# Twenty score passes of a unit, split as twelve and eight where other work follows

## The chip, the core and the metric

The program runs on one core of one Trainium2 chip. The metric is the device time of one launch in microseconds (us), the median of three runs. The profile comes from one more execution. The core has a TensorE (PE, with its weight loads listed as PEld), a VectorE (DVE), a ScalarE (ACT), a GpSimd (POOL) and a SyncE (SP) that issues most DMAs.

## The reference

Eight sequences of 1024 tokens with 256 channels go through a block of three layers, each added to its own input: half a feed-forward layer with eight routed experts, an attention layer, and the same feed-forward layer again. The attention is where the change lies.

```python
xd = (x @ W_down).reshape(b, t, h, s)              # 16 heads of 16 channels
keys    = einsum('bthk,hik->bthi', xd, tokeys) * scale
queries = einsum('bthk,hik->bthi', xd, toqueries) * scale
values  = einsum('bthk,hik->bthi', xd, tovalues)
dot  = einsum('bqhs,bkhs->bhqk', queries, keys)
attn = softmax(dot, axis=-1)
out  = einsum('bhqk,bkhs->bqhs', attn, values).reshape(b, t, e) @ W_unify + b_unify
...
x = x + 0.5 * ffn(layernorm(x))
x = x + attention(layernorm(x))
x = x + 0.5 * ffn(layernorm(x))
```

## The kernel before, in words

**Pairs and units.** `attention` works on 32 pairs: a pair is one sequence with one group of four heads. A pair has 16 units. A unit is one block of 512 queries with one block of 128 keys. The four heads of a group sit on the four strips of 32 rows of TensorE's array (`r = slice(32 * h, 32 * h + 32)`), so four matmuls, one in each strip, can run beside each other.

**Score passes.** In a unit, `passes` issues twenty matmuls of 512 columns (line 985). Each head has three "s" passes into a bank `psc` of PSUM: the high part of the keys, the low part, and one that subtracts the row maximum through `ones_r`. After the third, ScalarE takes the exponential of the bank into a tile `ex` (line 994). Each head also has two "m" passes into a bank `pm`. They are the scores of the next pair; VectorE reduces them to a maximum in `halves` (line 1001). Below, s0 to s3 and m0 to m3 name the bank and the pass by head; three passes in a row with the name s0 are the three passes of that bank.

**Order on TensorE.** The list `ORDERS` gives the twenty passes in two halves of ten: first `s0 s1 m2 m3 s0 s1 m2 m3 s0 s1`, then the same with `s2 s3 m0 m1`. Four names in a row that use four strips are a round. Each half is two whole rounds and a round of two.

**Weighing.** `weigh` multiplies the four `ex` tiles of the unit before with the values into one bank `av` (line 1016). These matmuls use all 128 rows and 32 columns each, so they cannot share the array with the strips. A weighing is done whole, between the two halves of passes, or in two parts of 256 columns: one between the halves, the other at the end.

**Other work.** `beside` is a list of generators that prepare the next sequence (`prepare`: transposes `ptan`, projections `pxd`, `pq`, `pv`), finish the last (`unify`: `pu`) and route it (`route`: transposes `ptrn`, logits `pl`, and in `places` the small matmuls `places` and `behind`). `run` advances them with `step`. In some units, by `SLOTS_OF`, it takes a step of kind `ARRAY` at the end of the unit, behind both halves; then `other` is true and the weighing is whole. This is called a mixed unit here, and any other a plain unit. 156 of the units are mixed: 28 with a `pu` step, 28 with `pxd`, 14 with `pq`, 14 with `pv`, 14 with `ptan`, 13 with `ptrn`, 24 with `pl`, 6 with `places`, 6 with `behind`, and 9 whose step issues nothing on TensorE. Ahead of 116 of them is a plain unit, ahead of the other 40 a mixed one.

**Banks.** `psc` and the tiles `ptan`, `ptrn`, `pxd`, `pq`, `pv` (by `bank`) share four PSUM banks. `pm`, `pu`, `pl`, `places` and `behind` (by `bank_v`) share three. A bank is taken in turn, and its first matmul waits for the reader of the tile that had it: ScalarE's `ex` or copy, or VectorE's reduction. TensorE, ScalarE and VectorE run their instructions in the order in which the kernel writes them (`tc.manual_schedule`); POOL and SP are scheduled by the tile layer.

The lines that decide what a unit does, in `run`:

```python
passes(n, n + 1, u, ORDERS[0], todo)
other = u % TB in slots[0] and due(ARRAY) is not None
whole = other or u % TB < 2
weighed((0, 1) if whole else (0,))
passes(n, n + 1, u, ORDERS[1], todo)
if other:
    step(ARRAY)
elif not whole:
    weighed((1,))
```

Of the kernel before, what the change touches and what calls it, by code (L numbers as in the profile page):

```python
# [40 lines left out]
def macaron(  # L41
# [714 lines left out]
    def reload(b):  # L756
        load_x(b, after_first.rearrange("(b t) d -> b t d", t=T))

    def attention(use, weights, router):
# [16 lines left out]
        ORDERS = [  # L776
            [(kind, int(h)) for kind, h in order.split()] for order in (
                "s0 s1 m2 m3 s0 s1 m2 m3 s0 s1", "s2 s3 m0 m1 s2 s3 m0 m1 s2 s3"
            )
        ]  # L780


        ORDER_OF_LAST = [("s", h) for _ in range(3) for h in range(4)]

        def bank(name):

            return use.sc.tile([P, 512], F32, tag="sc", name=name)

        def bank_v(name):

            return use.pm.tile([P, 512], F32, tag="pm", name=name)
# [125 lines left out]
        def fetch(n):  # L917

            b, g = divmod(n, G)
            rows = slice(g * 64, (g + 1) * 64)  # L920
            qt = qts[n] = use.pool.tile([P, T], F32R, tag=f"q{n % 3}", name=f"q_{n}")
            kt = kts[n] = use.pool.tile([P, 2, T], F32R, tag=f"k{n % 3}", name=f"k_{n}")
            for i in range(2):
                nc.sync.dma_start(
                    out=kt[:, i, :].bitcast(F32), in_=krows[b][i, rows].rearrange("r c t -> (r c) t")
                )
            nc.sync.dma_start(out=qt.bitcast(F32), in_=qrows[b][rows].rearrange("r c t -> (r c) t"))
# [26 lines left out]
        def passes(n, m, u, order, todo):  # L954

            q, c = divmod(u, TB)
            t, half = divmod(u, 2)
            qs, ks = slice(q * 512, (q + 1) * 512), slice(c * P, (c + 1) * P)  # L960

            def in_order(row):

                return row[:, qs].rearrange("p (t a j) -> p a t j", t=4, a=4)

            qm, km = slice(t * P, (t + 1) * P), slice(half * 512, (half + 1) * 512)
            for kind, h in order:
                if (n if kind == "s" else m) is None:
                    continue
                r = slice(32 * h, 32 * h + 32)  # L970
                if (kind, h) not in todo:
                    if kind == "s":
                        todo[kind, h] = bank(f"psc_{n}_{u}_{h}"), [
                            (kts[n][r, 0, ks], in_order(qts[n][r])),
                            (kts[n][r, 1, ks], in_order(qts[n][r])),
                            (ones_r[r, :], ms[(2 * n + q) % 4][r, :]),
                        ]
                    else:
                        todo[kind, h] = bank_v(f"pm_{m}_{u}_{h}"), [
                            (qts[m][r, qm], kts[m][r, i, km]) for i in range(2)  # L980
                        ]
                    todo[kind, h, "of"] = len(todo[kind, h][1])
                ps, left = todo[kind, h]
                lhs, rhs = left.pop(0)
                nc.tensor.matmul(  # L985
                    ps, lhsT=lhs, rhs=rhs,
                    start=(len(left) + 1 == todo[kind, h, "of"]), stop=not left,
                )
                if left:
                    continue  # L990
                if kind == "s":
                    ex = use.pool.tile([P, 512], F32, tag="ex", name=f"ex_{n}_{u}_{h}")

                    nc.scalar.activation(ex, ps, AF.Exp, scale=S ** -0.5)  # L994
                    todo["ex", h] = ex
                else:
                    if m not in halves:
                        halves[m] = use.pool.tile(
                            [P, TB, 2, 4], F32, tag="halves", name=f"halves_{m}"
                        )  # L1000
                    nc.vector.tensor_reduce(  # L1001
                        halves[m][:, t, half, h : h + 1], ps, AX.X, ALU.max, negate=True
                    )
# [3 lines left out]
        def weigh(n, u, exs, parts=(0, 1)):  # L1007

            b, g = divmod(n, G)
            q, c = divmod(u, TB)  # L1010
            if (n, q) not in avs:
                avs[n, q] = use.av.tile([P, 512], F32, tag="av", name=f"av_{n}_{q}")
            cols = slice(256 * parts[0], 256 * (parts[-1] + 1))
            for h, ex in enumerate(exs):
                at = (c * HEADS + 4 * g + h) * V
                nc.tensor.matmul(  # L1016
                    avs[n, q][32 * h : 32 * h + 32, cols],
                    lhsT=vps[b % 2][:, at : at + 2 * S],
                    rhs=ex[:, cols],
                    start=(c == 0),  # L1020
                    stop=(c == TB - 1 and parts[-1] == 1),
                )
            if c == TB - 1:
                divide(n, q)
# [90 lines left out]
        def stats(b):  # L1115

            sl = slice(b * TB, (b + 1) * TB)
            yield from norm_steps(f"a{b}", b, amean[:, sl], arstd[:, sl])
# [4 lines left out]
        def afterwards(n=0):  # L1123

            for _ in range(len(later) - n):
                later.pop(0)()
# [5 lines left out]
        def due(kind):  # L1132
            return min((w for w in beside if w[1] == kind), key=lambda w: w[0], default=None)
# [29 lines left out]
        def ones(i):  # L1163
            vp = use.pool.tile([P, TB * HEADS * V + S], F32, tag=f"vp{i}", name=f"vp{i}")
            nc.gpsimd.memset(vp, 1.0)
            vps.append(vp)

        def zero_rows(i):
            m = use.pool.tile([P, 512], F32R, tag=f"m{i}", name=f"m{i}")
            nc.gpsimd.memset(m.bitcast(F32), 0.0)  # L1170
            ms.append(m)
# [46 lines left out]
        def run(own):  # L1218
            for i in range(2, 4):
                zero_rows(i)  # L1220
            fetch(1)
            ones(1)
            for b in range(AHEAD - 1, B):
                reload(b)
                beside.append([G * (b - 1) - 1, DVE, stats(b)])
            last = None

            def weighed(parts=(0, 1)):
                if last is not None:
                    weigh(*last, parts=parts)  # L1230

            for n in range(PAIRS):
                ahead = n + 1 < PAIRS
                if n == (B - 1) * G:
                    done_by(n)
                    use.pool = own
                    use.last.close()
                    router.open()

                queue(n)  # L1240
                for u in range(UNITS):
                    todo = {}
                    old = len(later)
                    slots = SLOTS_OF[n % G < 2]
                    if ahead:
                        passes(n, n + 1, u, ORDERS[0], todo)

                        other = u % TB in slots[0] and due(ARRAY) is not None

                        whole = other or u % TB < 2  # L1250
                        weighed((0, 1) if whole else (0,))
                        passes(n, n + 1, u, ORDERS[1], todo)
                        if other:
                            step(ARRAY)
                        elif not whole:
                            weighed((1,))
                    else:

                        passes(n, None, u, ORDER_OF_LAST, todo)
                        weighed()  # L1260
                        other = False
                        if u > 1:
                            step(ARRAY)
                        if u == TB + 3:
                            beside.append([n + 1, ARRAY, islice(unify(B - 1), 2)])
                    if u % TB in slots[1]:
                        step(DVE)
                    if not other:
                        step(POOL)
                    last = (n, u, [todo["ex", h] for h in range(4)])  # L1270
                    afterwards(len(later) - old)
                    if ahead and u % TB == TB - 1:
                        lowest(n + 1, u // TB)
                if ahead:
                    done_by(n)
            weighed()
            afterwards()
            done_by(PAIRS + G)
            for _ in unify(B - 1, TB // 2):
                pass  # L1280
# [124 lines left out]
```

## Time and profile before

| what | value |
|---|---|
| time, median of 3 runs (lowest, highest) | 2952.49 us (2950.14, 2956.28) |
| time of the profiled execution | 2947.41 us |
| its span, first to last instruction | 2945.7 us |
| mean granted TensorE clock | 0.978 |
| busy: PE, PEld, DVE, ACT, POOL | 2805.4, 1549.6, 1879.2, 1375.5, 863.4 us |
| line 1001, reductions of `pm` | 2048, mean 681 ns |
| line 994, exponentials of `psc` | 2048, mean 596 ns |
| line 985, passes into `psc` (two kinds) and `pm` | 4096 + 2048 and 4096 |
| line 1016, weighings | 6472, mean 450 ns |

The profiled execution is 5.1 us below the median, and 1.7 us of its time lie outside the span. The mixed units begin between 670 and 2389 us of the span. The starts of matmuls are read from the trace; their ends are modelled, so the distance from one start to the next says more than a duration.

### The profile page before, as it was taken

How to read it: one execution, taken by the hardware profiler on the slowest of the kernel's cores; microseconds unless marked ns; L12 is line 12 of the kernel's file. 1: busy time of each engine (PE TensorE's matmuls, PEld its weight loads, DVE VectorE, ACT ScalarE, POOL GpSimd, SP SyncE). 2: the span in 40 equal slices, each digit the busy share in tenths (PEclk: the TensorE clock that was granted, in tenths of full speed). 3: DMA queues.
4: the chain of work that ended last, by engine and by line, in shares of the span. 5: the costliest groups of instructions: out<-in, count | busy, mean ns of one | idle time of the engine just before them, and what ended most of it. 6: DMA issues, size and time to landing. Idle time of an engine off the chain costs nothing.

```text
span 2945.7 us, 56665 instructions
## 1 busy us (share of the span) xinstructions
PE 2805.4 (95%) x22066; PEld 1549.6 (53%) x22066; DVE 1879.2 (64%) x4177; ACT 1375.5 (47%) x2512; POOL 863.4 (29%) x1144
## 2 busy tenths in 40 slices
PE   4799999899999999999999999999999998999998
PEld 4567776454444444444444444444444445666775
DVE  7344223567998888888888787788787963222221
ACT  1111111207666666766766766766765672111111
POOL 3444433314001034133123221321410215432331
PEclk7799999999999999999999999999999999999999
DMA  8522553415112101301301301301411102311440
GB/s 227 149 85 76 184 186 99 152 38 177 35 49 77 67 27 64 117 24 58 126 24 56 127 24 50 133 24 44 161 38 38 39 3 71 129 60 51 148 148 28
DMA packets 163736, 251.46 MB, mean 85 GB/s; under 512 B 36737, under 2 KB 109698, under 8 KB 163458
## 3 DMA queue, kind: packets, MB, share of 16 engines
q1 hardware_dynamic: 144178, 196.93, 20.6%
q0 software_dynamic: 18432, 50.62, 5.1%
q8 instruction: 177, 2.90, 0.4%
q14 instruction: 101, 0.83, 0.1%
q10 hardware_dynamic: 848, 0.18, 0.0%
HBM read 144.10 MB, written 103.57 MB: 84 GB/s over the span
## 4 chain that ended last, share of the span: by engine, by line
PE 63%; DVE 13%; issue 1%; POOL 1%; DMA 0%; ACT 0%; POOLq 0%; ACTq 0%
PE psc L985 19%; PE av L1016 15%; DVE halves L1001 9%; PE pm L985 7%; PE pe_o L499 5%; PE ph_o L456 5%; PE pe_e L499 2%; PE ph_e L456 2%; PE pu L1061 2%; PE pxd L860 2%; PE pv L892 1%; DVE turned L1031 1%; PE pq L878 1%; PE pl L1089 1%; PE ptrn L830 0%
## 5 line engine op out<-in xcount | busy, mean ns | idle before, releaser
L1001 DVE TENSOR_REDUCE halves<-pm 128x1 f32<-128x512 f32 x2048 | 1309.7, 681 | 258.1 <-PE pm L985 229.0
L994 ACT ACTIVATE ex<-psc 128x512 f32<-128x512 f32 x2048 | 1111.6, 596 | 579.1 <-PE psc L985 574.4
L985 PE MATMUL pm<-k,q 32*128 32x512 f32 x4096 | 872.5, 449 | 47.3 <-DVE halves L1001 38.0
L985 PE MATMUL psc<-q,k 32*128 32x512 f32 x4096 | 794.1, 456 | 2.9 <-PEq L668 2.9
L1016 PE MATMUL av<-ex,vp 128*32 128x256 f32 (+1 forms) x6472 | 614.2, 450 | 0.0
L985 PEld LDWEIGHTS psc<-q,k 32*128 32x128 f32 x4096 | 327.8, 183 | 480.5 <-issue 421.5
L985 PEld LDWEIGHTS pm<-k,q 32*128 32x128 f32 x4096 | 375.5, 184 | 129.8 <-DVE halves L1001 107.1
L985 PE MATMUL psc<-m,ones_r 32*128 32x512 f32 x2048 | 407.9, 390 | 0.0
L456 PE MATMUL ph_o<-bT_o,oa 128*128 128x512 f32 x704 | 321.9, 607 | 9.6 <-DVE h_o L474 8.5
L499 PE MATMUL pe_o<-ob,h_o 128*128 128x256 f32 x1408 | 318.6, 382 | 0.0
L1039 POOL TENSOR_TENSOR ot<-turned,rec 128x256 f32<-128x256 f32 x64 | 39.6, 619 | 886.6 <-DVE rec L1034 880.1
L499 PEld LDWEIGHTS pe_o<-ob,h_o 128*128 128x128 f32 x1408 | 265.5, 191 | 47.2 <-issue 13.5
L1016 PEld LDWEIGHTS av<-ex,vp 128*32 128x32 f32 x6472 | 129.0, 108 | 299.3 <-issue 276.3
L456 PEld LDWEIGHTS ph_o<-bT_o,oa 128*128 128x128 f32 x704 | 133.1, 194 | 164.1 <-issue 149.8
L470 ACT ACTIVATE h_o<-ph_o,ob 128x512 f32<-128x512 f32 x88 | 60.4, 687 | 338.7 <-PE ph_o L456 319.5
L474 DVE TENSOR_SCALAR h_o<-ph_o,ob 128x512 f32<-128x512 f32 x88 | 66.0, 750 | 230.4 <-ACT h_o L470 226.0
L985 PEld LDWEIGHTS psc<-m,ones_r 32*128 32x128 f32 x2048 | 197.7, 185 | 13.3
L509 DVE SCALAR_TENSOR_TENSOR y_o<-pe_o,old_o 128x256 f32<-128x256 f32 x88 | 37.2, 423 | 195.2 <-PE pe_o L499 195.1
L499 PE MATMUL pe_e<-wb,h_e 128*128 128x256 f32 (+1 forms) x640 | 143.9, 381 | 0.0
L456 PE MATMUL ph_e<-bT_e,wa 128*128 128x320 f32 x512 | 140.6, 433 | 1.8 <-ACT bT_e L204 1.8
L204 ACT COPY bT_o<-pt_bT_o 128x1024 f32<-128x1024 f32 x22 | 22.3, 1012 | 241.2 <-PE pt_bT_o L200 241.2
L499 PEld LDWEIGHTS pe_e<-wb,h_e 128*128 128x128 f32 (+1 forms) x640 | 112.9, 179 | 16.4 <-issue 3.1
(181 smaller groups left out, 2395.8 us busy)
## 6 DMA issues: line engine op xcount, KB each, us to landing
k<-krows SPq DMA_DIRECT2D x64, 512.0 KB
wa<-in_w_dram SPq DMA_DIRECT2D x16, 1024.0 KB
wb<-in_w_dram SPq DMA_DIRECT2D x16, 1024.0 KB
krows<-kh SPq DMA_DIRECT2D x32, 512.0 KB
krows<-kl SPq DMA_DIRECT2D x32, 512.0 KB
q<-qrows SPq DMA_DIRECT2D x32, 512.0 KB
rows_o<-buf SPq DMA_DIRECT2D x88, 130.0 KB
x<-in_x_dram SPq DMA_DIRECT2D x8, 1024.0 KB
```

The lines of the kernel that those rows point to most:

```text
L456: nc.tensor.matmul(ps[:, i * 512 : i * 512 + width], lhsT=wa[:, k, (m + i) * P : (m + i + 1) * P], rhs=xnt[:, k, c0:c1], start=(k == 0), s ...
L470: nc.scalar.activation(t[:, 0, : hi - lo], ps[:, lo - c0 : hi - c0], AF.Relu, bias=bias[:, m : m + 1],)
L474: nc.vector.tensor_scalar(t[:, 1, : hi - lo], ps[:, 512 + lo - c0 : 512 + hi - c0], bias[:, m + 1 : m + 2], 0.0, ALU.add, ALU.max,)
L499: nc.tensor.matmul(ps[lo - i * P : hi - i * P, :D], lhsT=of[:, lo - a : hi - a], rhs=w[:, m, :], start=(m == 0), stop=(m == MC - 1),)
L509: nc.vector.scalar_tensor_tensor(y[:n, :], ps[:n, :D], 0.5, olds[i][:n, :], ALU.mult, ALU.add)
L860: nc.tensor.matmul(ps, lhsT=wd_sb[:, k, m * P : (m + 1) * P], rhs=xnt[:, k, :], start=(k == 0), stop=(k == KC - 1),)
L985: nc.tensor.matmul(ps, lhsT=lhs, rhs=rhs, start=(len(left) + 1 == todo[kind, h, "of"]), stop=not left,)
L994: nc.scalar.activation(ex, ps, AF.Exp, scale=S ** -0.5)
L1001: nc.vector.tensor_reduce(halves[m][:, t, half, h : h + 1], ps, AX.X, ALU.max, negate=True)
L1016: nc.tensor.matmul(avs[n, q][32 * h : 32 * h + 32, cols], lhsT=vps[b % 2][:, at : at + 2 * S], rhs=ex[:, cols], start=(c == 0), stop=(c == ...
L1039: nc.gpsimd.tensor_tensor(outs_t[q][:, :, at : at + S].rearrange("p (t a) s -> p a t s", t=4), by[:, :, :S].rearrange("p (a t) s -> p a t ...
L1061: nc.tensor.matmul(ps[:, i * D : (i + 1) * D], lhsT=outs[b, g, q][:, at : at + P], rhs=wu_sb[:, g, :], start=(g == 0), stop=(g == G // 2 - 1),
```

## The change

Mixed units get an order list of their own. Their first half has twelve passes in three rounds of four strips, their second half eight passes in two rounds; the whole weighing stays between the halves and the step behind them. The order in plain units stays. `other` is now worked out ahead of the first half, because the choice of the list needs it; nothing in between changes what it depends on.

```diff
+        ORDERS_WITH_OTHER = [
+            [(kind, int(h)) for kind, h in order.split()] for order in (
+                "s2 s3 m0 m1 s2 s3 m0 m1 s2 s3 s0 s1", "s0 s1 m2 m3 s0 s1 m2 m3"
+            )
+        ]
...
                     if ahead:
-                        passes(n, n + 1, u, ORDERS[0], todo)
 
                         other = u % TB in slots[0] and due(ARRAY) is not None
+                        orders = ORDERS_WITH_OTHER if other else ORDERS
+                        passes(n, n + 1, u, orders[0], todo)
 
                         whole = other or u % TB < 2
                         weighed((0, 1) if whole else (0,))
-                        passes(n, n + 1, u, ORDERS[1], todo)
+                        passes(n, n + 1, u, orders[1], todo)
```

## The prediction

> **What bounds the kernel now.** I read the page, the busy times by stretch and then the timeline of single units. Attention fills 655 to 2396 us:
>
> ```profile
> 655.00:2396.00 1741.00, 1696.71 (x17253) 787.07 (x17255) 1451.50 (x2855) 1168.39 (x2170) 423.18 (x517) 0.99 0.20 68
> ```
>
> The columns after the length are PE, PEld, DVE, ACT and POOL, then clock, DMA share and GB/s. TensorE is busy 97% of it, DVE 83%, ACT 67%. So TensorE sets the pace, but its busy time hides rounds that fill two strips. The timeline of a plain unit's end and a mixed unit with a `pu` step shows them:
>
> ```profile
> 1115.54 1.08 ACT L994 ACTIVATE ex<-psc 128x512 f32<-128x512 f32 x2 [0.76 <-PE psc L985]
> 1115.91 0.51 PE L985 MATMUL psc<-q,k 32*128 32x512 f32 x2
> 1116.25 0.39 PE L985 MATMUL psc<-q,k 32*128 32x512 f32 x1
> 1116.49 0.39 PE L985 MATMUL psc<-m,ones_r 32*128 32x512 f32 x2
> 1116.81 1.06 PE L1016 MATMUL av<-ex,vp 128*32 128x512 f32 x8
> 1117.80 0.50 PE L985 MATMUL psc<-q,k 32*128 32x512 f32 x2
> 1118.14 0.40 PE L985 MATMUL psc<-q,k 32*128 32x512 f32 x1
> 1118.38 0.39 PE L985 MATMUL psc<-m,ones_r 32*128 32x512 f32 x2
> 1118.70 1.13 PE L1061 MATMUL pu<-wu,ho 128*128 128x256 f32 x4
> ```
>
> The unit begins at 1115.91. Start to start: first round 0.34, second 0.24, third (two strips) 0.32, then the weighing 0.99; the second half again 0.34, 0.24, 0.32; then the step. The first round costs 0.11 more than the second because its weights aren't in yet; 0.32 is a round and the change to another shape of tile. From the unit's begin to its step: 0.90 + 0.99 + 0.90 = 2.79. Also to be seen: the last two exponentials of the plain unit before end at 1115.54 + 1.08 = 1116.62, which is 0.71 into the mixed unit. Over the 116 mixed units behind a plain one this end has the median 0.68, and in 112 of them it lies between 0.65 and 0.75.
>
> **What the change removes.** The work on TensorE is the same, packed in five rounds instead of six. With all banks free the first half stays 0.34 + 0.24 + 0.32 = 0.90 (its last round is full now), and the second half is 0.34 + 0.32 = 0.66. Saved: 0.24 us a mixed unit; in 156 units at most 37 us.
>
> **What it adds: an earlier wait.** s0 and s1 now open their banks in the third round, 0.58 into the unit, instead of s2 and s3 behind the weighing at 1.89. The build of the changed program gives s0 and s1 the banks of the plain unit's s2 and s3, and s1's wait is for the fourth exponential of that unit. In the kernel before it was the weighing, at 0.90, that asked for that exponential first. What such a wait costs is seen where one stands:
>
> ```profile
> 1092.51 1.29 DVE L1001 TENSOR_REDUCE halves<-pm 128x1 f32<-128x512 f32 x2 [0.49 <-PE pm L985]
> ...
> 1093.86 0.18 PEld L985 LDWEIGHTS pm<-k,q 32*128 32x128 f32 x1 [0.42 <-DVE halves L1001]
> 1093.86 0.50 PE L985 MATMUL psc<-q,k 32*128 32x512 f32 x2
> ...
> 1094.20 0.39 PE L985 MATMUL psc<-m,ones_r 32*128 32x512 f32 x2
> 1094.52 0.16 PEld L1016 LDWEIGHTS av<-ex,vp 128*32 128x32 f32 x8 [0.37 <-issue]
> ```
>
> The reductions end at 1093.80 and the weight load of the waiting pass starts 0.06 later, not before; the next round starts 0.34 after that, not 0.23. So a pass that waited pays 0.11 for weights that weren't loaded ahead. In the changed unit: s1's load at 0.68 + 0.055 = 0.735 (a waiting pass starts 0.05 to 0.06 behind its reader wherever one stands in the trace), its stream at 0.845, the weighing 0.315 after that, at 1.16 instead of 0.90: +0.26. The second half begins at 2.15, the step at 2.15 + 0.66 = 2.81 against 2.79. A gain of 0.24 becomes a loss of about 0.03. Queued behind the waiting s1 on TensorE is the whole weighing, and behind that m2 and m3, so VectorE's second pair of reductions comes 0.26 late.
>
> Two rules of the Trainium skill bear on this. "TensorE: Matmul & The Clock Gate", Part 2, says that the queue pulls weight loads ahead of matmuls in flight; if that held for a pass that waits, the 0.11 would fall away and the sum below would be near 0. In the rows above the load starts with the release, so I keep the 0.11. "TensorEngine Tiling (Array Packing)", Performance Considerations, warns that packing speeds up TensorE but not the emptying of PSUM; by it alone a denser unit gains nothing, a sum of 0 at best.
>
> **The sum by kind of unit** (length of the step, and what the next unit waits for, from the timeline of each kind):
>
> - 63 units behind a plain one with a long step (21 `pu`, 22 `pxd`, 7 `pq`, 13 `pv`; steps of 1.92 to 1.98). The late reductions end 4.23 into the unit, the next unit begins at 4.7: hidden. 63 x 0.03 = +1.9.
> - 26 with transposes (1.03). Before, the next unit's s1 waits for the last exponential, its load 4.10 into the unit; now for that of s1, whose last pass starts at 2.15 + 0.34 = 2.49 instead of 2.47. 26 x 0.025 = +0.7.
> - 6 with `places` (0.45). The fence above is the unit behind one: it stands until the last reduction. That reduction is 0.26 late now: +1.6.
> - 21 with `pl` or nothing on TensorE. Here too the next unit stands on the reductions, but those stand behind a division (`turned`, `rec`) that ends after the late pair is there; it moves by some 0.04. +0.8.
> - 14 of the 40 behind a mixed unit, whose step took a bank for `pxd` or `pq`. The changed program gives s1 that bank. Its reader is the second of ScalarE's copies:
>
> ```profile
> 722.54 0.50 PE L985 MATMUL psc<-q,k 32*128 32x512 f32 x2
> 722.69 0.59 ACT L846 CAST kh<-pxd 128x512 fp32r<-128x512 f32 x1 [0.78 <-POOL ot L1039]
> 723.17 0.59 ACT L847 COPY xd<-pxd 128x512 f32<-128x512 f32 x1
> 723.44 0.16 PEld L1016 LDWEIGHTS av<-ex,vp 128*32 128x32 f32 x8 [0.37 <-PE pm L985]
> ```
>
>   The unit begins at 722.54, the copy ends at 723.76, 1.22 in. s1's load at 1.275, the weighing at 1.275 + 0.43 = 1.70 instead of 0.90: +0.80, less 0.24: +0.56. Before, the banks of these copies were asked for at 1.89, when they were done. 14 x 0.56 = +7.8.
> - 7 `pu` behind `pu`: all banks free. 7 x -0.24 = -1.7.
> - 19 behind a mixed unit with `pl`, `behind` or one `ptan`: both ends, their own and the next unit's begin, hang on reductions that keep their distance. 0.
>
> Together 1.9 + 0.7 + 1.6 + 0.8 + 7.8 - 1.7 = **+11.1 us**. Against the profiled execution: 2947.4 + 11.1 = 2958.5; that one is 5.1 below the median, so the median goes from 2952.5 to **2963.6 us**, slower by 0.4%. About 0.2% (6 us) is what a measurement of this kernel can tell from no change. POOL and SP keep their queues but for two neighbouring stores, DMAs aren't added, and the exponentials of s2 and s3 come when those of s0 and s1 came: these edits are costed at nothing under TensorE's unit.
>
> The unknown is the price of the wait in 116 + 14 units. Below: no weight penalty, 0.11 less where it counts (63 + 26 + 6 + 14), -12 us. Above: rounds that start up to 0.1 later behind a wait in the same 109 units, +11.
>
> **Rivals.**
>
> - *The banks are free in time* (the change does what it says). Then the weighing stays at 0.90: 63 x -0.24, 26 x -0.24, 14 x -0.24 and 7 x -0.24; the units on reductions gain nothing. -26 us, 2926. For it: only TensorE's busy 97%. Against it: the 0.68, which would have to fall to about 0.4 in the first pass that needs the bank. It decides from there.
> - *The weight load isn't exposed.* The wait stays, 0.15 instead of 0.26. 2952, no change. For it: it is one row's reading carried from a `pm` in a first round to a `psc` in a third. Against: each waiting load in that view has the same form.
> - *Reductions decide more often.* The 0.26 isn't hidden behind the division in the 21 units, and the 19 that follow lose it too: 40 x 0.2 = +8, 2972. For it: VectorE is at 83% and the next units already stand on it. Against: the order of the division, which ends last there now.
>
> **How the numbers follow.** Forecast 0.62, free banks 0.12, no weight penalty 0.13, more reductions 0.13. The forecast's lower edge reaches into "no change": 0.06 of its 0.62. Faster 0.12; within 0.2% 0.13 + 0.06 = 0.19; slower 0.56 + 0.13 = 0.69. The range takes the second and third rival and the upper bound, and leaves out the free banks: 2949 to 2976.
>
> **What would show it.** In the timeline after, a mixed unit behind a plain one: second half of 0.66 instead of 0.90, and the weighing near 1.16 instead of 0.90, with s1's weight load released by `ex`. In the waits of PEld, `psc` on `ex` grows from 38.5 us, and a new one on `xd` or `kh` appears in the units behind `pxd`. If the weighing still starts at 0.90, the step of the wait is wrong and the time falls to 2926; if it starts at 1.05, only the 0.11 is wrong.

## The result, and the profile after

The changed kernel takes 2969.48 us (median of 6 runs, 2962.71 to 2975.71), the kernel before 2950.77 us beside it (6 runs, 2948.97 to 2956.28). The ratio is 1.006 with a 95% interval of 1.0044 to 1.0077: slower by 13 to 23 us. The profiled execution took 2973.0 us with a span of 2971.3.

The busy times of the attention stage, in the same columns as before:

```profile
664.00:2423.00 1759.00, 1710.23 (x17257) 788.27 (x17255) 1453.76 (x2855) 1169.44 (x2170) 423.68 (x517) 0.99 0.19 67
```

The stage is 18 us longer (1759 against 1741) with the same work on every engine. TensorE shows 13.5 us more busy time with the same number of matmuls (17257 against 17253, a few records fall on the edges): the time went into longer records (of passes that waited, and of some at half clock, see the last section), not into more work.

The mixed unit with a `pu` step whose timeline was shown of before begins at 1129.20 in the timeline after. These are the rows that the reading needs, with those between left out, as in all timelines below:

```profile
1128.76 1.09 ACT L1001 ACTIVATE ex<-psc 128x512 f32<-128x512 f32 x2 [0.70 <-PE psc L992]
1129.20 0.50 PE L992 MATMUL psc<-q,k 32*128 32x512 f32 x2
1129.55 0.40 PE L992 MATMUL psc<-q,k 32*128 32x512 f32 x2
1129.78 0.39 PE L992 MATMUL psc<-q,k 32*128 32x512 f32 x1
1129.90 0.18 PEld L992 LDWEIGHTS psc<-q,k 32*128 32x128 f32 x1 [0.16 <-ACT ex L1001]
1129.90 0.49 PE L992 MATMUL psc<-q,k 32*128 32x512 f32 x1
1130.33 1.07 PE L1023 MATMUL av<-ex,vp 128*32 128x512 f32 x8
1131.32 0.50 PE L992 MATMUL psc<-q,k 32*128 32x512 f32 x2
1131.66 0.39 PE L992 MATMUL psc<-m,ones_r 32*128 32x512 f32 x2
1131.99 0.70 PE L1068 MATMUL pu<-wu,ho 128*128 128x256 f32 x2
```

The exponentials of the plain unit end at 1129.85, s1's weight load starts at 1129.90, 0.70 into the unit (the line with PEld and `ex`; s1's pass is the line below it), and the weighing at 1130.33, 1.13 in. The second half is 0.67 long. The step comes at 2.79 into the unit, where it came before. The gain of a round is there, and the wait for s1's bank has eaten it.

Behind a `pxd` step the bank is the one that ScalarE's copy reads:

```profile
731.67 0.50 PE L992 MATMUL psc<-q,k 32*128 32x512 f32 x2
732.30 0.59 ACT L854 COPY xd<-pxd 128x512 f32<-128x512 f32 x1
732.95 0.18 PEld L992 LDWEIGHTS psc<-q,k 32*128 32x128 f32 x1 [0.75 <-ACT xd L854]
733.38 0.16 PEld L1023 LDWEIGHTS av<-ex,vp 128*32 128x32 f32 x8 [0.24 <-issue]
```

The load stands until 1.28 into the unit, the weighing starts at 1.71. In the list of PEld's waits the wait for `ex` grew from 38.5 us in 61 cases to this, and one on `xd` is new:

```profile
PEld psc L992 <- ACT ex L1001: 48.9, 135, 0.8
PEld psc L992 <- ACT xd L854: 9.4, 13, 0.7
```

### The profile page after: what moved, and what is told of

It is laid out like the page before. It is cut to its first block, busy times and chain, and to the rows that moved or that the text cites. A ratio compares the mean times of both kernels' runs of the same rounds, so it can differ in the third digit from the quotient of the medians.

```text
span 2971.3 us, 56354 instructions
## 1 busy us (share of the span) xinstructions
PE 2828.5 (95%) x22066; PEld 1558.8 (52%) x22066; DVE 1881.5 (63%) x4177; ACT 1375.9 (46%) x2512; POOL 861.9 (29%) x1144
## 4 chain that ended last, share of the span: by engine, by line
PE 54%; DVE 12%; POOL 5%; issue 5%; ACT 0%; DMA 0%; POOLq 0%; DVEq 0%; ACTq 0%
PE psc L992 16%; PE av L1023 12%; DVE halves L1008 9%; PE pm L992 6%; PE pe_o L499 5%; PE ph_o L456 5%; PE pe_e L499 2%; PE ph_e L456 2%; PE pu L1068 2%; POOL buf L361 1%; POOL send L184 1%; DVE turned L1038 1%; PE pxd L867 1%; POOL an L184 1%; PE pv L899 1%
## 5 line engine op out<-in xcount | busy, mean ns | idle before, releaser
L992 PE MATMUL psc<-q,k 32*128 32x512 f32 x4096 | 835.7, 460 | 7.0 <-ACT xd L854 3.7
L992 PEld LDWEIGHTS psc<-q,k 32*128 32x128 f32 x4096 | 363.6, 184 | 513.5 <-issue 428.0
L456 PE MATMUL ph_o<-bT_o,oa 128*128 128x512 f32 x704 | 321.8, 607 | 11.1 <-DVE h_o L474 8.6
```

The costliest lines, as they stand in the source:

```text
L456: nc.tensor.matmul(ps[:, i * 512 : i * 512 + width], lhsT=wa[:, k, (m + i) * P : (m + i + 1) * P], rhs=xnt[:, k, c0:c1], start=(k == 0), s ...
L992: nc.tensor.matmul(ps, lhsT=lhs, rhs=rhs, start=(len(left) + 1 == todo[kind, h, "of"]), stop=not left,)
```

## The experiments

The runs of one kernel spread by 6 to 30 us, so besides the medians I compare the units one by one: the length of a unit is from its first pass to the next unit's first pass, and for each kind of unit I take the median change against the first trace of before, times the number of such units. The sum of these for the changed kernel is +15.1 us.

**The order of before behind `prepare`.** The list is chosen with one more condition:

```diff
-                        orders = ORDERS_WITH_OTHER if other else ORDERS
+                        orders = ORDERS_WITH_OTHER if other and behind != "prepare" else ORDERS
+                        behind = due(ARRAY)[2].__name__ if other else None
```

> The changed kernel, but the 14 mixed units that stand behind a mixed unit with a pxd or pq step keep the order of before. My theory (s1's bank there is the one that ScalarE still copies from): these 14 units lose 0.56 us each with the new order, so this runs 7.8 us faster than the changed kernel, about 2962 against 2969.5. In the trace their weighing starts at 0.90 into the unit again instead of at 1.66 to 1.71. Rival (the loss lies in the 116 units behind a plain one): no change, 2969.

Measured: 2959.93 us, 1.0047 of before (1.0021 to 1.0073). By kinds of units the sum falls from +15.1 to +6.2; the 14 units alone go from +7.8 to 0. Their weighing starts at 0.90 again. The theory holds for them. The two medians alone could not settle it, since this interval and that of the changed kernel (1.0044 to 1.0077) overlap; by the lengths of the units the rival fails: these 14 units carry half of the loss.

**The order of before behind `route`.** The same edit with `"route"`. It reaches fewer units than the expectation says: only the 12 `pl` units behind a `pl` unit. The other 7 of the 19 stand behind a step that issues nothing on TensorE, which is the last, empty step of `unify`; in this run's trace they still have twelve passes ahead of the weighing.

> The changed kernel, but the 19 mixed units behind a mixed unit with a step of route (pl, or one that issues nothing on TensorE) keep the order of before. New theory from the trace after: in these units m1 waits for a reduction in the first round, and the full third round has a pass of m1's own strip, so that wait reaches the weighing 0.23 later; the next unit, which stands on the reductions too, is late with it. 12 units with pl behind pl cost some 0.09 + 0.27 each, so this runs about 4.3 us faster than the changed kernel, 2965; with 8 or more the stretch at half clock in the profile was no accident. As the prediction had it (these units keep their distances): no change, 2969.

Measured: 2964.98 us, 1.0062 (1.0040 to 1.0084), 4.5 below the changed kernel, which these intervals alone can't tell from it. By kinds the sum is +12.0. The 12 units and the units after them go from +4.3 to +1.2: the units after them lost 0.27 each in the changed kernel and lose nothing here, and the 12 themselves take 0.10 more than before in both. (The 19 with what follows them go from +4.7 to +1.4.) So they do not keep their distances, as the prediction had it. The 12 units' weighing has the median 1.31 before, 1.64 in the changed kernel and 1.41 here: 0.23 of the delay is the order's, and 0.10 comes from the unit ahead, which has the new order in this run too. The first round of such a unit, with the reduction it waits for, is in the timeline after:

```profile
1063.68 0.50 PE L992 MATMUL psc<-q,k 32*128 32x512 f32 x2
1064.43 0.18 PEld L992 LDWEIGHTS pm<-k,q 32*128 32x128 f32 x1 [0.41 <-DVE halves L1008]
1064.79 0.60 PE L992 MATMUL psc<-q,k 32*128 32x512 f32 x2
1065.32 0.16 PEld L1023 LDWEIGHTS av<-ex,vp 128*32 128x32 f32 x8 [0.36 <-PE psc L992]
```

and in the timeline of before:

```profile
1053.36 0.18 PEld L985 LDWEIGHTS pm<-k,q 32*128 32x128 f32 x1 [0.41 <-DVE halves L1001]
1053.71 0.40 PE L985 MATMUL psc<-m,ones_r 32*128 32x512 f32 x2
1054.04 0.16 PEld L1016 LDWEIGHTS av<-ex,vp 128*32 128x32 f32 x8 [0.37 <-PE pm L985]
```

From the released load to the weighing it is 0.68 before and 0.89 after. Before, the third round had two passes on strips 0 and 1, and the pass that waited was m3's on strip 3: two rounds of that strip follow the wait. After, m1 waits on strip 1, and the full third round has s1 on strip 1 too: three rounds follow it. (The line with 0.60 holds s0 and s1; s1 starts 0.21 behind s0.) The half-filled third round had been a cushion for such waits. The next unit, which stands on reductions, takes 0.27 more in the changed kernel.

**Eight and twelve.** The wait for the bank is moved behind the weighing, the five rounds stay:

```diff
-                "s2 s3 m0 m1 s2 s3 m0 m1 s2 s3 s0 s1", "s0 s1 m2 m3 s0 s1 m2 m3"
+                "s2 s3 m0 m1 s2 s3 m0 m1", "s2 s3 s0 s1 s0 s1 m2 m3 s0 s1 m2 m3"
```

> The five rounds stay, but they go as eight and twelve around the whole weighing: s2 s3 m0 m1 twice, the weighing, then s2 s3 s0 s1, s0 s1 m2 m3 twice. s0 and s1 ask for their banks behind the weighing, when they are free. My theory (the packing is worth 0.24 us a unit and the earlier wait for s1's bank eats it): the weighing starts near 0.70 (it needs the fourth exponential at 0.735), the step 2.63 into the unit instead of 2.79. 63 x -0.16, 26 x -0.17, 6 x +0.07, 21 x -0.24 for those behind prepare and unify, the others about 0: -19 us against the kernel before, 2932. Rival (full rounds take longer or bring the clock down, so that five cost as much as six): 2950 or more.

Measured: 2970.47 us, 1.0077 (1.0054 to 1.0100); by kinds +18.5. The sum missed by 38 us. Full rounds are not dearer: units with a `pu` step behind a plain one are 0.16 shorter, as expected, and their weighing starts at 0.73. But those with `pxd` are 0.16 longer, those with transposes 0.22. The timeline of one with `pxd`:

```profile
1169.97 0.50 PE L992 MATMUL psc<-q,k 32*128 32x512 f32 x2
1170.71 1.06 PE L1023 MATMUL av<-ex,vp 128*32 128x512 f32 x8
1171.70 0.50 PE L992 MATMUL psc<-m,ones_r 32*128 32x512 f32 x2
1172.30 1.57 ACT L1001 ACTIVATE ex<-psc 128x512 f32<-128x512 f32 x3 [1.64 <-PE psc L992]
1172.95 0.30 PEld L867 LDWEIGHTS pxd<-Tan,wd 128*128 128x128 f32 x2 [0.71 <-ACT ex L1001]
```

The tile `pxd` takes the oldest of the four banks, that of s2. s2 now gets its third pass behind the weighing, its exponential (the first of the three in the line) ends at about 1172.89, and the step's first weight load stands until 1172.95, 2.98 into the unit instead of 2.63. The same holds for the other steps that take one of these four banks: the step's first load starts 0.05 behind the end of that exponential in the median with `pxd`, `pq` and `pv`, and 0.04 with the transposes. My expectation had counted the banks of the passes and forgotten the step's own. That is 27 of the 38 us (63 units: +3.5 instead of -10.1; 26 units: +8.8 instead of -4.4). Most of the rest lies in the 21 units with `pl` or no step (+2.0 instead of -5.0) and the 19 of the second experiment with the units after them (+3.7 instead of 0); no run looks into its cause.

**The order of before behind every mixed unit.** The first edit with `behind is None`.

> The changed kernel, but all 40 mixed units behind a mixed one keep the order of before; the 116 behind a plain one have the new order. My theory: in those 116 the gain of the packing and the price of the wait cancel to within some 3 us, so this is at 2951 + 3 = 2954. Rival (the wait is what makes the kernel slower in the units behind a plain one): it stays near 2965 to 2969. Rival (the packing gains where the other losses are gone): 2930 to 2945.

Measured: 2957.10 us, 1.0032 (1.0016 to 1.0048): 5 to 14 us above before. By kinds +4.4, of which +0.3 lie in the 63 units with a long step, +0.4 in the 26 with transposes, +1.8 in and behind those with `places` and +2.1 in those with `pl` or no step. So in the 116 units gain and wait cancel to within 4.6 us, a little more than the 3 of the first theory. By the sum by kinds neither rival holds; the interval alone would just touch the first. The 19 units and those after them are at -0.2 here and +4.7 in the changed kernel, so their loss comes from their own order; the 0.10 of the 12 `pl` units stays.

**Before, once more.**

> The kernel before once more, for a second trace of it: where the stretches at half clock fall, and how long the stage ahead of the attention takes. If that stage takes 662 to 667 us here too (658.8 in the first trace), the changed kernel's 667 there is no effect of the change.

Measured: 2947.94 us. The attention starts at 663.7 us here and at 658.8 in the first trace; in the changed kernel and the other variants it starts between 658.7 and 667.5. The code ahead of the attention is the same in all of them, and kernels with a changed attention lie at both ends (658.7 and 667.5), so nothing here points to the change as the cause of the 667.4. The second trace of before did reach the 662 to 667 that I had named. From the first pass of the first unit to that of the last the two traces of before differ by 4.4 us (1789.9 and 1785.5), while the sum by kinds differs by 0.3.

**Eight and twelve where it fits.** Only units with `pu`, `pxd` or `pv` get the list of the third experiment; `coming` is a note of what the generator does next:

```diff
-                    ps = bank(f"pxd_{b}_{m}_{q}")
+                    ps = bank_v(f"pxd_{b}_{m}_{q}")
...
-                    ps = bank(f"pv_{b}_{t}")
+                    ps = bank_v(f"pv_{b}_{t}")
...
+                        of = due(ARRAY)[2].__name__ if other else None
+                        orders = EIGHT_TWELVE if of == "unify" and coming["pu"] or (
+                            of == "prepare" and coming["an"] in ("pxd", "pv")
+                        ) else ORDERS
```

> Eight passes, the whole weighing, twelve passes, but only in the 70 mixed units with a pu, pxd or pv step; the tiles of pxd and pv move to the three banks of bank_v; all other units keep the order of before. My theory of the miss of the eight-and-twelve run (the step's tile takes the bank of s2, whose exponential now comes late, and stands 0.33): with the tile elsewhere the units with pxd and pv take 0.16 to 0.22 less than before, as those with pu did there. 28 + 28 + 14 units, -12 us, 2936 against 2948. Rival (the units with pxd and pv are slow for another reason, the order itself): they stay 0.16 above those of before, and the sum is about 0 to +2.

Measured: 2934.01 us, 0.9950 of before (0.9932 to 0.9968); by kinds -12.3. It is faster than both kernels. The same `pxd` unit in its timeline:

```profile
1151.61 0.50 PE L998 MATMUL psc<-q,k 32*128 32x512 f32 x2
1152.34 1.06 PE L1029 MATMUL av<-ex,vp 128*32 128x512 f32 x8
1153.34 0.50 PE L998 MATMUL psc<-m,ones_r 32*128 32x512 f32 x2
1154.24 0.30 PEld L870 LDWEIGHTS pxd<-Tan,wd 128*128 128x128 f32 x2 [0.36 <-issue]
```

The step starts 2.63 into the unit and waits for nothing but the array. That shows two things. A packed round is worth 0.15 to 0.23 a unit where no bank stands in its way: the units behind a plain one are 0.15 to 0.16 shorter and the `pu` units behind `pu` 0.22. And in the units with `pxd` and `pv` the miss of the third experiment was the step's bank. No run moves the tiles to `bank_v` under the old order. But the `pu` units, whose bank did not move, gain the same 0.16, and before the change no load of `pxd` or `pv` in the attention stood for a bank, so the move alone had nothing to remove there.

**Asking a round earlier.** The five rounds of the changed kernel in another order:

```diff
-                "s2 s3 m0 m1 s2 s3 m0 m1 s2 s3 s0 s1", "s0 s1 m2 m3 s0 s1 m2 m3"
+                "s2 s3 m0 m1 s2 s3 s0 s1 s2 s3 m0 m1", "s0 s1 m2 m3 s0 s1 m2 m3"
```

> Twelve and eight as in the changed kernel, same five rounds, but the first half is s2 s3 m0 m1, s2 s3 s0 s1, s2 s3 m0 m1: s0 and s1 ask for their banks one round earlier. My theory (the wait is for the plain unit's last exponential at 0.735, whenever the bank is asked for, and what stands behind it in the strip comes 0.34 later): the weighing starts at 1.39 instead of 1.16, each unit behind a plain one takes about 0.25 more than in the changed kernel and those behind pxd or pq as much: some +45 us against the kernel before, 2993. Rival (five rounds cost what they cost, in any order): 2965 to 2970.

Measured: 2994.69 us, 1.0154 (1.0123 to 1.0186); by kinds +45.4. The timeline of the same `pu` unit:

```profile
1126.34 1.09 ACT L1001 ACTIVATE ex<-psc 128x512 f32<-128x512 f32 x2 [0.71 <-PE psc L992]
1126.77 0.50 PE L992 MATMUL psc<-q,k 32*128 32x512 f32 x2
1127.48 0.18 PEld L992 LDWEIGHTS psc<-q,k 32*128 32x128 f32 x1 [0.31 <-ACT ex L1001]
1127.49 0.71 PE L992 MATMUL pm<-k,q 32*128 32x512 f32 x2
1128.13 0.16 PEld L1023 LDWEIGHTS av<-ex,vp 128*32 128x32 f32 x8 [0.36 <-issue]
```

The load is released at 0.71 into the unit (0.70 in the changed kernel); a round of the same strip comes behind it, and the weighing starts at 1.36 (median over these units 1.39). The same twenty passes in the same five rounds cost 30 us more than in the changed kernel (+45.4 against +15.1) because a bank is asked for one round earlier.

## Why the prediction was right, and where its sum was off

The direction and the mechanism held, step by step. s1's load waits for the fourth exponential of the plain unit: predicted 0.735, measured medians 0.67 to 0.75 by kind of unit, each 0.05 behind the end of that exponential. The weighing: predicted 1.16, measured 1.10 to 1.18. The weight load of the waiting pass is not hidden: in every kind of unit where s1 waited, the weighing starts 0.43 behind s1's load, as the 0.11 + 0.315 of the prediction had it. Its matmul's record is 0.49 long in the `pu` unit, against 0.38 to 0.39 for its three neighbours. The rival without that price would have had the weighing at 1.05, and the free banks would have had it at 0.90. Part 2 of "TensorE: Matmul & The Clock Gate" in the Trainium skill tells of weight loads that are pulled ahead of matmuls in flight. It does not help a pass that itself waits here: in the waits shown the load starts 0.05 to 0.06 behind the end of the reader, never ahead of it.

The terms of the sum, against the medians by kind in the trace after:

| units | predicted | measured |
|---|---|---|
| 63 long steps behind a plain unit | +1.9 | +0.9 |
| 26 with transposes | +0.7 | -0.3 |
| 6 with `places` | +1.6 | +1.5 |
| 21 with `pl` or no step | +0.8 | +2.2 |
| 14 behind `pxd` or `pq` | +7.8 | +7.8 |
| 7 `pu` behind `pu` | -1.7 | -1.6 |
| 19 behind a mixed unit with a `pl` step or one that issues nothing on TensorE, and the units after them | 0 | +4.7 |
| sum | +11.1 | +15.1 |

The median moved by 18.7 us. The term of the sum that was mis-sized is the last one of the table, put at 0 and measured at +4.7: "reductions that keep their distance" holds for the reduction and the pass that it releases, but not for what stands behind that pass in its own strip. This is close to the third rival in size and place, though mostly not by its cause: the division still hid the late pair at the end of the `pl` units (their own length grew by 0.03), and the two timelines beside the second experiment put 0.21 on the strip. A smaller part is of the rival's kind: the 0.10 that a `pl` unit behind a `pl` unit takes more, 1.2 us in 12 units, passes on from the unit ahead, and it is gone where that unit has the order of before. The 40 units of the two terms together lost 6.9 us, where that rival, with its 8 on top of the 0.8, had 8.8.

Of the 21 units the nine whose step issues nothing on TensorE are 0.21 longer. Before, nothing stood between the half-filled round at their end and the next unit's first passes: from the weighing to the next unit it was 1.57, that is 0.99 + 0.34 + 0.24, without a third round, and it is 1.57 after. So packing that round away saved nothing in them, and the wait remained. Seven of the nine are followed by a mixed unit that stands on reductions anyway and is 0.19 shorter for it, so 1.3 of these 1.9 us come back in the term of the 19.

So the +11.1 is not as close to +15.1 in its parts as the mechanism is: two terms came out lower by 2.0 us together, two higher by 6.1, and these partly cancel. What lies between 15.1 and 18.7 is within the interval of the measurement (13 to 23). Single executions differ through the clock too: between the two traces of before it made some 4.5 us, by the measure of the last section.

## What to carry to other kernels

When a half-filled round is packed with work from later, look up which buffer that work opens and who frees it. The earlier request has to be set against the time at which the reader ends, not against the engine that looks busy, and it has to be done for every tile in the rotation, the one of the step behind included. A half-filled round can be a cushion for a wait on another strip: here the time from the release to the weighing was 0.68 with it and 0.89 without. So pack the rounds in those units where the buffers are free, by kind of unit, and leave the rest.

## What the runs showed that I had not expected

In each trace the granted clock falls to 0.50 for short stretches within the attention, 3 to 14 us at a time. In all nine traces one of 6.8 us begins 0.4 to 1.5 us behind the first pass of the first unit; the others come at other places in each execution. Together they add up to 6.8 to 34.1 us of a trace between the first and the last unit (23.9 and 13.7 in the two traces of before, 34.1 in that of the changed kernel). The busy times of the changed kernel just ahead of one and in it, in the columns given above:

```profile
1968.00:1981.00 13.00, 12.90 (x150) 6.27 (x142) 11.59 (x22) 9.19 (x18) 6.52 (x7) 1.00 0.34 121
1982.00:1995.00 13.00, 13.00 (x86) 5.94 (x80) 6.13 (x11) 5.22 (x10) 0.00 (x0) 0.50 0.01 3
```

In the same 13 us TensorE starts 86 matmuls instead of 150. A `pl` unit that a stretch falls on took 6.40 us instead of 4.29, the median of its kind. Beyond the medians of their kinds, the units that a stretch falls on took 12.6 us in the trace after, 9.1 in the first trace of before and 4.6 in the second. That is some 3.5 us of the difference between the two profiled executions, an estimate by this measure. From the first pass of the first unit to that of the last they differ by 18.1 us, and the sum by kinds is 15.1 of it. Whether the packing brings on more of these stretches stays open: the fastest variant had 27.3 us of them, the third experiment 17.1.
